# Opening stage of a two-layer AdaLN block: gates broadcast through DRAM, rows turned back into their own buffers, 64-column modulation matmuls, another batch order

## The chip, the core and the metric

The kernel runs on one core of a Trainium2 chip. The core has a matrix engine (TensorE; its matmuls are "PE" and its weight loads "PEld" in the profile), a vector engine (VectorE, DVE), an activation engine (ScalarE, ACT), a general engine (GpSimd, POOL) and a queue processor (SyncE, SP). Each engine executes its own instructions in their order and waits on semaphores for the others. Data lie in an on-chip memory of 128 partitions (SBUF), matmul results in an accumulator memory (PSUM), of which this kernel uses eight banks in three pools of 3, 2 and 3. Transfers between DRAM and SBUF are issued by an engine's queue (SPq, ACTq, POOLq) and carried out by DMA engines.

The metric is device time in microseconds, the median of several runs. The profile is one further execution.

## What is computed

Two layers, each with two branches. A branch normalises its input, scales and shifts it by values that depend on the batch (the modulation), applies an operator, and adds the result times a gate to the input. Batch 4, sequence 1024, width 256, all fp32. Cut to what matters here, layer 0:

```python
mod = (_silu(L0_c) @ L0_wmod).reshape(L0_c.shape[0], 6, 1, -1)
sa, ca, ga, sb, cb, gb = (mod[:, 0], mod[:, 1], mod[:, 2], mod[:, 3], mod[:, 4], mod[:, 5])
ga = (2 * (ga >= 0) - 1) * jnp.maximum(jnp.abs(ga), 0.25)
gb = (2 * (gb >= 0) - 1) * jnp.maximum(jnp.abs(gb), 0.25)
h = _layernorm(x, axis=-1) * (1 + ca) + sa
x = x + ga * _L0_attn_ref(h, L0_attn_queries, L0_attn_combiners)
h = _layernorm(x, axis=-1) * (1 + cb) + sb
x = x + gb * _L0_ffn_ref(h, L0_ffn_W1, ...)
```

The attention has no softmax and four heads of 64. Per head and batch it is `h (Q (h^T h) C)`, so that it can be computed from the 64 x 64 Gram matrix `h^T h` of each head:

```python
Q = jnp.einsum('btae,aeqf->qbtaf', x, qw)
pre = jnp.einsum('qbtaf,buqf->qbtau', Q, x)
attn = jnp.einsum('qbtau,buqg->abtqg', pre, x)
out = jnp.einsum('abtk,akg->btag', attn, combiners)
```

The feed-forward part of layer 0 routes each token to the best two of eight experts. Layer 1 has a gated fast-weight product in place of the attention and a routed linear layer. They follow the stage that is changed and are not touched.

## The kernel before

The program has two recorded parts. The first is **phase A**: the attention of layer 0, the second normalisation, the router logits, and the tables that say which rows go to which expert. The rest is the expert blocks of layer 0 and all of layer 1. Phase A is written as pieces handed to a planner (`class Plan`, L39): each piece names its engine, an expected duration, what it follows, the buffers ("slots") that it holds and a rank. `Plan.run` (L61) lists them in the order of begin times that it works out, and that order becomes each engine's instruction order. So an engine's order is fixed before the run, from the planner's durations, ranks and slot counts (L858), and not by what really finishes first.

Tokens lie as `x_sb[128, 8, batch, 256]`: eight tiles of 128 tokens for each batch. A *group* is four tiles; a batch has two groups. For each batch:

* **First half** (`first_half`, L1060, at rank `FIRSTS[b]`). For each group: statistics on DVE (L942, L943), a square root on ACT (L950), a Newton step of five small DVE instructions (L954 to L961), the normalised rows `xn` on ACT (L968). PE turns them to features (`to_features`, `pm_t`, L1008); ACT applies the modulation by feature on the way out of PSUM (L1013, `h1T`). PE turns that back to tokens (`to_tokens`, `pm_b`, L1035), and ACT copies it to `h` (L1040), a buffer of its own (`h1` in this half, `h2` in the second). The Gram matrix of the batch (`pm_gram`, L1102) needs both groups of `h`. Then come two short products: DVE copies the diagonal blocks (`gd`, L1112), PE makes `pm_t1` (L1134), ACT copies it (L1144), PE makes `pm_m` (L1155), and DVE multiplies that by the gate `ga0` into `md` (L1167).
* **Second half** (`second_half`, L1183, at rank `SECONDS[b]`). PE makes the attention's output `pm_o` from `h1T` and `md` (L1195), DVE adds it to `x_sb` (L1205), and the normalisation runs again with the second modulation, giving `h2T`. PE makes the router logits `pm_l` (L1235), DVE chooses the experts (`route`, L394, L1253), PE turns `h2T` back, ACT copies it to `h`, and SP stores it to `h_rows` in DRAM (L1270), from where the expert blocks gather rows. One batch (`SPLIT`) is routed in two pieces.

**Modulation.** `mods_by_feature` (L874) makes the four shift and scale vectors with one matmul for each 128 features and half of the contraction, with four moving columns (one for each batch), from `sT`, the silu of the conditioning vector (`silu_of`, L308). The two gates are made as rows on four partitions (`gate_row`, L901). Since `ga0` and `gb0` are needed on all 128 partitions, `gates` (L917) then multiplies the rows by a selector `pick` (L250): for each batch one matmul of 4 x 512 (`spread`, L332, the instruction is L335), and two ACT copies out of PSUM (L927, L928).

**SP's queue** in phase A: the eight loads of x (L218) with the small weights between them, the first two sets of expert weights (L236, L237), a filler row of `h_rows` (L853), the second layer's modulation weights (`load_wm1`, L1307), filler rows for later tables, then the eight stores of `h_rows`. ACT's queue loads the modulation weights of layer 0.

**The end of phase A**: when all router logits are there, PE turns the choices (`turn`, L434), DVE builds the block tables (L562, L667), GpSimd gathers the first rows (L348), and the first expert matmul (L1609) starts.

Of the kernel before, what the change touches and what calls it, by code (L numbers as in the profile page):

```python
# [8 lines left out]
F32 = mybir.dt.float32  # L9
F16 = mybir.dt.float16  # L10
I32 = mybir.dt.int32
AF = mybir.ActivationFunctionType
# [11 lines left out]
E = 8  # L24
# [113 lines left out]
def adaln_d2_kernel(  # L138
# [92 lines left out]


    w1buf = [pw.tile([P, W1ROW], F32, name=f"w1_{i}") for i in range(2)]
    w2buf = [pw.tile([P, W2ROW], F32, name=f"w2_{i}") for i in range(2)]
    for i in range(2):
        nc.sync.dma_start(w1buf[i], W1[(E - 1) * P :, :])  # L236
        nc.sync.dma_start(w2buf[i], W2[(E - 1) * P :, :])  # L237

    xgbuf = [pw.tile([P, D], F32, name=f"xg_{i}") for i in range(4)]
# [7 lines left out]
    for e in range(E):  # L247
        nc.gpsimd.memset(rank[:, e : e + 1], float(E - e))

    pick = pa.tile([B, B, P], F32, name="pick", bufs=1)  # L250
    nc.gpsimd.memset(pick, 0.0)
    nc.gpsimd.affine_select(
        out=pick,
        in_=pick,
        compare_op=ALU.not_equal,
        fill=1.0,
        base=0,
        pattern=[[-1, B], [0, P]],
        channel_multiplier=1,
    )  # L260
    ones16 = const.tile([P, P], F16, name="ones16")
# [46 lines left out]
    def silu_of(layer, cT):  # L308
        sT = small.tile([P, KD, B], F32, name=f"sT{layer}")
        nc.scalar.activation(sT, cT, AF.Silu)  # L310
        return sT

    def mod_rows(sT, w, at, n):

        pr = psum(ps_2, [B, n], "pm_mod")
        for k in range(KD):
            nc.tensor.matmul(
                pr, lhsT=sT[:, k, :], rhs=w[:, k, at : at + n], start=(k == 0), stop=(k == KD - 1)
            )
        return pr  # L320

    def gate_of(dst, src, scratch):
# [7 lines left out]
        nc.vector.scalar_tensor_tensor(dst, sign, -1.0, size, ALU.add, ALU.mult)  # L330

    def spread(b, rows):  # L332

        pb = psum(ps_m, [P, rows.shape[1]], "pm_bc")
        nc.tensor.matmul(pb, lhsT=pick[:, b, :], rhs=rows, start=True, stop=True)  # L335
        return pb

# [500 lines left out]

    modT = const.tile([P, 4, KD, B], F32, name="modT")
    SA, CA, SB, CB = range(4)  # L840
# [16 lines left out]

    plan = Plan(p1=3, p2=2, pm=3, xn1=3, h1T=2, h1=1, xn2=2, h2T=2, h2=4, t1=1)  # L858
    PE, ACT, DVE, POOL = "PE", "ACT", "DVE", "POOL"
# [14 lines left out]
    def mods_by_feature(which, column, at):  # L874
        ps = plan.slot("p1")

        def mm():
            pf = tiles["modT", which] = psum(ps_1, [P, 2 * KD, B], "pm_modT")
            for i in range(2):
                for q in range(KD):  # L880
                    c = column[i] * D + q * P
                    for k in range(KD):
                        nc.tensor.matmul(
                            pf[:, i * KD + q, :],
                            lhsT=wm0[:, k, c : c + P],
                            rhs=sT0[:, k, :],
                            start=(k == 0),
                            stop=(k == KD - 1),
                        )

        def out_():
            pf = tiles["modT", which]
            nc.vector.tensor_copy(modT[:, which[0], :, :], pf[:, :KD, :])
            nc.vector.tensor_scalar(
                modT[:, which[1], :, :], pf[:, KD:, :], 1.0, None, ALU.add
            )

        i = plan(PE, 1.8, mm, holds=[ps], at=at, rank=-1)
        return plan(DVE, 0.4, out_, after=[i], holds=[ps], rank=-1)

    def gate_row(i, column, at):  # L901
# [13 lines left out]
        )  # L915

    def gates(after):  # L917
        done = []
        for b in range(B):
            ps = plan.slot("pm")  # L920

            def mm(b=b):
                tiles["spread", b] = spread(b, gate_rows.rearrange("b i d -> b (i d)"))

            def out_(b=b):
                pb = tiles["spread", b]
                nc.scalar.copy(ga0[:, b, :], pb[:, :D])  # L927
                nc.scalar.copy(gb0[:, b, :], pb[:, D:])  # L928

            m = plan(PE, 0.9, mm, after=after, holds=[ps], rank=b - 0.4)  # L930
            done.append(plan(ACT, 0.8, out_, after=[m], holds=[ps], rank=b - 0.4))
        return done

# [65 lines left out]
    def to_features(b, g, key, slot, dst, held, shift, scale, after, rank):  # L999

        done = []
        for k in range(KD):
            ps = plan.slot("pm")

            def mm(k=k):
                pt = tiles["pt", key, k] = psum(ps_m, [P, 4, P], "pm_t")
                for i in range(4):
                    nc.tensor.transpose(  # L1008
                        pt[:, i, :], tiles["xn", key][:, i, k * P : (k + 1) * P], ident
                    )  # L1010

            def out_(k=k):
                nc.scalar.activation(  # L1013
                    dst()[:, k, :, :],
                    tiles["pt", key, k],
                    AF.Identity,
                    bias=modT[:, shift, k, b : b + 1],
                    scale=modT[:, scale, k, b : b + 1],
                )

            m = plan(PE, 0.55, mm, after=after, holds=[ps, slot, held], rank=rank)
            done.append(plan(ACT, 0.67, out_, after=[m], holds=[ps, held], rank=rank))
        return done

    def to_tokens(key, src, held, dst, to, after, rank):

        done = []
        for i in range(2):
            ps = plan.slot("pm")

            def mm(i=i):
                pb = tiles["pb", key, i] = psum(ps_m, [P, 2, D], "pm_b")
                for q in range(2):
                    for k in range(KD):
                        nc.tensor.transpose(  # L1035
                            pb[:, q, k * P : (k + 1) * P], src()[:, k, 2 * i + q, :], ident
                        )

            def out_(i=i):
                nc.scalar.copy(dst()[:, 2 * i : 2 * i + 2, :], tiles["pb", key, i])  # L1040

            m = plan(PE, 0.55, mm, after=after, holds=[ps, held, to], rank=rank)
            done.append(plan(ACT, 0.6, out_, after=[m], holds=[ps, to], rank=rank))
        return done
# [12 lines left out]

    FIRSTS, SECONDS, SPLIT = [0.0, 1.89, 1.82, 2.75], [1.66, 2.89, 3.45, 2.92], 2

    def first_half(b, arrival):  # L1060

        rank = FIRSTS[b]
        held, to = plan.slot("h1T"), plan.slot("h1")
        hT = buffer(("h1T", b), "h1T", [P, KD, NC, P])
        h = buffer(("h1", b), "h1", [P, NC, D])
        whole = []
        for g in range(2):
            key, slot = (1, b, g), plan.slot("xn1")
            n = normalised(
                b, range(4 * g, 4 * g + 4), key, slot, lambda c: [], rank, arrival[g]  # L1070
# [13 lines left out]
            )  # L1084
            whole += to_tokens(
                key,
                lambda cs=cs: hT()[:, :, cs, :],
                held,
                lambda cs=cs: h()[:, cs, :],
                to,  # L1090
                f,
                rank,
            )

        ps, gd, md = plan.slot("p1"), gds[b % 2], mds[b % 2]

        def gram(j, cs):
            if j == 0 and cs[0] == 0:
                tiles["gram", b] = psum(ps_1, [P, KD, P], "pm_gram")
            for c in cs:  # L1100
                hj = h()[:, c, j * P : (j + 1) * P]
                nc.tensor.matmul(  # L1102
# [12 lines left out]
        for j in range(KD):  # L1115
            for cs in (range(4), range(4, NC)):
# [5 lines left out]
                        after=m,  # L1122
                        holds=[ps, to],
                        rank=rank,
# [38 lines left out]
        def head_m_out():  # L1163
# [12 lines left out]
            head_m_out,  # L1176
            after=[m, gates0[b], *before],
            holds=[ps],
# [4 lines left out]
    def second_half(b):  # L1183
# [34 lines left out]
        for g in range(2):  # L1218
# [25 lines left out]
            if b == SPLIT:  # L1244
                of_batch["routed"] = ready[g][0]
            h2, to = buffer(("h2", b, g), "h2", [P, 4, D]), plan.slot("h2")
            backs[g] = (to_tokens(key, hT2, held2, h2, to, f, rank + 0.1), to, h2)
        for gs in routed:
# [16 lines left out]
            for g in gs:  # L1265
                back, to, h2 = backs[g]

                def store(g=g, h2=h2):
                    at = 4 * g * B * P
# [3 lines left out]
                        )[b],  # L1273
                        h2(),
                    )

                plan("SP", 4.0, store, after=back, holds=[to], rank=rank)

# [6 lines left out]
    rows_done = [gate_row(0, 2, 10.0), gate_row(1, 5, 12.0)]  # L1285
    gates0 = gates(rows_done)
    for b in range(B):
# [21 lines left out]

    loaded = plan("SP", 0.3, load_wm1, after=[mods_a, mods_b, *rows_done])  # L1310
    for piece in range(3):
        ps = plan.slot("p2")
        m = loaded
        for k in range(KD):

            def mm(piece=piece, k=k):
                if k == 0:
                    tiles["rows1", piece] = psum(ps_2, [B, 2 * D], "pm_mod")
                nc.tensor.matmul(
                    tiles["rows1", piece],  # L1320
                    lhsT=sT1[:, k, :],
                    rhs=tiles["wm1"][:, k, 2 * D * piece : 2 * D * (piece + 1)],
# [1145 lines left out]
```

## Time and profile before

| | us |
|---|---|
| runs, median of 3 | 1163.62 |
| runs, lowest and highest | 1161.59, 1166.54 |
| profiled execution, its own time | 1162.08 |
| its span, first to last instruction | 1160.3 |
| first Gram copy (L1112) starts | 33.51 |
| last router call of phase A (L1235) ends | 110.42 |
| first expert matmul (L1609) starts | 126.32 |

The span is the part of the profiled execution between its first and last instruction; 1.8 us lie around it. "Busy" is the time in which an engine had an instruction under way. For PE it says nothing of how fast: the granted clock of PE stands beside it, 1.00 being full speed. Its mean over this execution is 0.984. An instruction's row gives start, length, engine, line, operation, output and inputs, their shapes, how many were merged into the row, and, in brackets, how long the engine stood idle before it and what released it. A matmul of fp32 operands appears as two records, an fp32 transpose as one.

### The profile page before, as it was taken

The page shows a single profiled execution, that of the slowest core. Times are in us where ns is not written, and L with a number is a line of the kernel's source. Part 1 is how long each engine was busy: PE and PEld are TensorE (multiplying, and loading weights), DVE is VectorE, ACT ScalarE, POOL GpSimd, SP SyncE. Part 2 cuts the span into 40 slices and gives each one's busy share as a digit, 9 for nine tenths or more (in the row PEclk, how much of TensorE's full clock was granted, in tenths as well). Part 3 has the DMA queues.
Part 4 walks back from the last instruction along what each step waited for, and adds up shares of the span by engine and source line. Part 5 has one row for each costly group of instructions (what it writes and reads, how often), then busy time and mean ns, then how long its engine had stood idle before and what let it go on. Part 6 is the DMA issues. An engine that isn't in the chain of part 4 may idle for free. (4 is left out here: it accounts for less than half of the span.)

```text
span 1160.3 us, 18416 instructions
## 1 busy us (share of the span) xinstructions
PE 1109.2 (96%) x6244; PEld 875.8 (75%) x6244; DVE 586.3 (51%) x2243; ACT 427.4 (37%) x1156; POOL 412.1 (36%) x479
## 2 busy tenths in 40 slices
PE   9999899999999999999989999999999999999893
PEld 5997799999999999999978455665657676646651
DVE  6686333322222222222244589878587535787566
ACT  4967233223233333333224333423324325342421
POOL 2000344444333344334464452420124332545544
PEclk7999999999999999999998999999999999999997
DMA  9203323655431415151251211110013323332534
GB/s 342 107 31 110 140 80 110 223 174 186 152 126 50 175 38 191 37 178 51 70 190 51 64 56 55 55 37 19 0 37 103 111 71 98 105 122 91 142 103 129
DMA packets 78305, 122.13 MB, mean 105 GB/s; under 512 B 23610, under 2 KB 62016, under 8 KB 73604
## 3 DMA queue, kind: packets, MB, share of 16 engines
q0 software_dynamic: 31680, 69.61, 19.3%
q1 hardware_dynamic: 45428, 49.75, 12.7%
q10 hardware_dynamic: 1104, 1.58, 0.4%
q8 instruction: 52, 0.85, 0.3%
q14 instruction: 41, 0.34, 0.1%
HBM read 204.13 MB, written 30.57 MB: 202 GB/s over the span
## 5 line engine op out<-in xcount | busy, mean ns | idle before, releaser
L1621 ACT ACTIVATE hid<-p_h,w 128x128 f32<-128x128 f32 x544 | 155.1, 368 | 339.6 <-issue 266.6
L1609 PEld LDWEIGHTS p_h<-xT,w 128*128 128x128 f32 x2176 | 255.3, 193 | 7.1 <-DVE xT L1594 3.3
L1609 PE MATMUL p_h<-xT,w 128*128 128x128 f32 x2176 | 256.8, 277 | 3.5 <-DVE xT L1594 2.9
L1632 PE MATMUL p_y<-w,hid 128*128 128x256 f32 x1088 | 252.1, 384 | 3.2 <-issue 3.2
L1906 PE MATMUL p_u<-hT,a 128*128 128x512 f32 x512 | 230.9, 595 | 1.7 <-issue 1.0
L348 POOL DMA_INDIRECT w<-in_W,g_wrow x134 | 133.8, 998 | 271.4 <-ACT hid L1621 130.3
L1632 PEld LDWEIGHTS p_y<-w,hid 128*128 128x128 f32 x1088 | 203.0, 192 | 29.4 <-issue 4.4
L1906 PEld LDWEIGHTS p_u<-hT,a 128*128 128x128 f32 x512 | 94.2, 190 | 98.2 <-issue 90.6
L1594 DVE COPY xT<-pm_x 128x256 f32<-128x256 f32 x68 | 28.8, 424 | 187.3 <-PE pm_x L1589 176.5
L1954 PE MATMUL p_f<-a,hf 128*128 128x256 f32 x512 | 116.6, 380 | 2.4 <-DVE step L1995 1.6
L1643 DVE TENSOR_TENSOR y<-p_y,w 128x256 f32<-128x256 f32 x68 | 28.8, 424 | 176.4 <-PE p_y L1632 176.4
L348 POOL DMA_INDIRECT xg<-h_rows,g_row x68 | 65.7, 966 | 130.9 <-DVE g_hits L752 110.5
L1954 PEld LDWEIGHTS p_f<-a,hf 128*128 128x128 f32 x512 | 95.9, 190 | 20.8 <-issue 5.9
L348 POOL DMA_INDIRECT yg<-y,g_slot x64 | 61.3, 959 | 85.9 <-DVE x_sb L1466 33.5
L2215 PE MATMUL p_e<-ew,xT 128*128 x280 | 70.3, 384 | 0.3 <-ACT y L2225 0.3
L348 POOL DMA_INDIRECT xg<-ga_rows,ga_row x39 | 37.2, 954 | 91.6 <-DVE ga_row L761 35.0
L1918 ACT ACTIVATE hf<-p_u,decay 128x512 f32<-128x512 f32 x56 | 38.0, 683 | 72.3 <-PE p_u L1906 68.2
L2215 PEld LDWEIGHTS p_e<-ew,xT 128*128 128x128 f32 x280 | 49.5, 190 | 10.4 <-issue 4.9
L1529 DVE TENSOR_TENSOR h<-h,mod 128x256 f32<-128x256 f32 x128 | 51.4, 425 | 9.2 <-ACT h L1519 6.3
L1922 DVE SCALAR_TENSOR_TENSOR hf<-p_u,decay,hf 128x512 f32<-128x512 f32 x56 | 41.9, 748 | 20.9 <-PE p_u L1906 13.4
L2225 ACT COPY y<-p_e 128x256 f32<-128x256 f32 x70 | 25.9, 371 | 57.0 <-PE p_e L2215 24.3
L2002 POOL TENSOR_TENSOR x_sb<-x_sb,step 128x256 f32<-128x256 f32 x32 | 23.8, 743 | 62.1 <-DVE step L1995 44.5
(368 smaller groups left out, 1296.8 us busy)
## 6 DMA issues: line engine op xcount, KB each, us to landing
y<-y SPq DMA_DIRECT2D x68, 128.0 KB
ga_y<-y SPq DMA_DIRECT2D x39, 128.0 KB
x_sb<-in_x SPq DMA_DIRECT2D x8, 512.0 KB
h_rows<-h SPq DMA_DIRECT2D x8, 512.0 KB
gb_y<-y SPq DMA_DIRECT2D x31, 128.0 KB
out_x<-x_sb SPq DMA_DIRECT2D x7, 512.0 KB
a<-in_fw SPq DMA_DIRECT2D x6, 512.0 KB
mod<-mod_rows SPq DMA_DIRECT2D x6, 512.0 KB
```

The source lines that it names most:

```text
L348: return nc.gpsimd.indirect_dma_start(out=dst, out_offset=None, in_=table, in_offset=bass.IndirectOffsetOnAxis(ap=index, axis=0), bounds_c ...
L1529: nc.vector.tensor_tensor(h, h, mods1[(sc, sh)[i]][:, b, :], (ALU.mult, ALU.add)[i])
L1594: nc.vector.tensor_copy(xT, pt)
L1609: nc.tensor.matmul(p1[:, i, :], lhsT=w1[:, k * H + m * P : k * H + (m + 1) * P], rhs=xT[:, k, :], start=(k == 0), stop=(k == KD - 1),)
L1621: nc.scalar.activation(hid[:, m, :], p1[:, i, :], AF.Relu, bias=w1buf[j % 2][:, KD * H + m : KD * H + m + 1],)
L1632: nc.tensor.matmul(p2, lhsT=hid[:, m, :], rhs=w2[:, m * D : (m + 1) * D], start=(m == 0), stop=(m == KH - 1),)
L1643: nc.vector.tensor_tensor(y, p2, w2buf[j % 2][:, KH * D :], ALU.add)
L1906: nc.tensor.matmul(pu, lhsT=a[:, k, m * P : (m + 1) * P], rhs=made["n1", c, "hT"][:, k, :, :], start=(k == 0), stop=(k == KD - 1),)
L1918: nc.scalar.activation(made[key, m], made[key, m, 0], AF.Silu, scale=decays[c])
L1922: nc.vector.scalar_tensor_tensor(h, made[key, m, 1], decays[c], h, ALU.mult, ALU.mult)
L1954: nc.tensor.matmul(made[key, "p2", b], lhsT=made[key, m][:, b * P : (b + 1) * P], rhs=a1[:, m, :], start=(m == 0), stop=(m == KH - 1),)
L2215: nc.tensor.matmul(made[key, "p2"], lhsT=made[key, "xT"][:, k, :], rhs=ew_flat[:, bass.ds(made[key, "at"] + k * D, D)], start=(k == 0), st ...
```

## The change

It has four parts, all in phase A. (a) The gate rows are no longer multiplied by a selector: SP stores the four gate rows to a small DRAM tensor `gates0` and loads them back with the same row for all partitions, first `ga0`, and later `gb0`. The loads of the expert weights, which stood ahead of the plan, become a piece of the plan behind the load of `ga0`, and the second layer's modulation weights come behind them. In the built SP queue, the first of the four weight loads stands between the store and the load of `ga0`, the other three behind it, then `gb0`. (b) The rows turned back to tokens are written into the `xn` buffer that they came from, and the `h1` and `h2` buffers go; `xn1` has five buffers in place of three, `xn2` six in place of two. (c) `sT` is padded with zeros to 64 columns and the modulation matmuls of `mods_by_feature` move all 64; the four that matter are read. (d) The ranks of the batches' halves change, and the batch that is routed in two pieces is 3 in place of 2.

```diff
-    for i in range(2):
-        nc.sync.dma_start(w1buf[i], W1[(E - 1) * P :, :])
-        nc.sync.dma_start(w2buf[i], W2[(E - 1) * P :, :])
...
-    pick = pa.tile([B, B, P], F32, name="pick", bufs=1)
-    nc.gpsimd.memset(pick, 0.0)
-    nc.gpsimd.affine_select(
...
     def silu_of(layer, cT):
-        sT = small.tile([P, KD, B], F32, name=f"sT{layer}")
-        nc.scalar.activation(sT, cT, AF.Silu)
+        sT = pa.tile([P, KD, ROUTER], F32, name=f"sT{layer}", bufs=1)
+        nc.vector.memset(sT, 0.0)
+        nc.scalar.activation(sT[:, :, :B], cT, AF.Silu)
         return sT
...
-    modT = const.tile([P, 4, KD, B], F32, name="modT")
+    modT = const.tile([P, 4, B, KD], F32, name="modT")
+    gates0 = dram.tile([B, 2, D], F32, name="gates0")
...
-    plan = Plan(p1=3, p2=2, pm=3, xn1=3, h1T=2, h1=1, xn2=2, h2T=2, h2=4, t1=1)
+    plan = Plan(p1=3, p2=2, pm=3, xn1=5, h1T=2, xn2=6, h2T=2, t1=1)
...
-            pf = tiles["modT", which] = psum(ps_1, [P, 2 * KD, B], "pm_modT")
+            pf = tiles["modT", which] = psum(ps_1, [P, 2 * KD, ROUTER], "pm_modT")
...
-    def gates(after):
-        done = []
-        for b in range(B):
-            ps = plan.slot("pm")
-
-            def mm(b=b):
-                tiles["spread", b] = spread(b, gate_rows.rearrange("b i d -> b (i d)"))
-
-            def out_(b=b):
-                pb = tiles["spread", b]
-                nc.scalar.copy(ga0[:, b, :], pb[:, :D])
-                nc.scalar.copy(gb0[:, b, :], pb[:, D:])
...
             def out_(i=i):
-                nc.scalar.copy(dst()[:, 2 * i : 2 * i + 2, :], tiles["pb", key, i])
+                nc.scalar.copy(tiles["xn", key][:, 2 * i : 2 * i + 2, :], tiles["pb", key, i])
...
-    FIRSTS, SECONDS, SPLIT = [0.0, 1.89, 1.82, 2.75], [1.66, 2.89, 3.45, 2.92], 2
+    FIRSTS, SECONDS, SPLIT = [0.0, 1.27, 2.12, 2.24], [1.14, 3.78, 2.27, 3.07], 3
...
-                hj = h()[:, c, j * P : (j + 1) * P]
+                hj = tiles["xn", (1, b, c // 4)][:, c % 4, j * P : (j + 1) * P]
...
-            after=[m, gates0[b], *before],
+            after=[m, gate_loaded, *before],
...
-    gates0 = gates(rows_done)
+
+    def gates_out():
+        nc.sync.dma_start(gates0, gate_rows)
+
+    def gate_in(i, dst):
+        nc.sync.dma_start(dst, gates0[:, i, :].partition_broadcast(P))
+
+    q = plan("SP", 0.1, gates_out, after=rows_done, rank=-0.8, lag=2.2)
+    gate_loaded = plan("SP", 0.1, lambda: gate_in(0, ga0), after=[q], rank=-0.8, lag=3.5)
+
+    def first_weights():
+
+        for i in range(2):
+            nc.sync.dma_start(w1buf[i], W1[(E - 1) * P :, :])
+            nc.sync.dma_start(w2buf[i], W2[(E - 1) * P :, :])
+        gate_in(1, gb0)
+
+    weights0 = plan("SP", 0.5, first_weights, after=[gate_loaded])
...
-    loaded = plan("SP", 0.3, load_wm1, after=[mods_a, mods_b, *rows_done])
+    loaded = plan("SP", 0.3, load_wm1, after=[weights0])
```

## The prediction

> **What bounds the kernel now.** First the page's busy table: TensorE (PE) is busy for 96% of the span, so the question is what its busy time is made of in the stretch that the change touches, the opening attention stage ("phase A"), which ends where the first expert matmul starts.
>
> ```profile
> PE 1109.2 (96%) x6244; PEld 875.8 (75%) x6244; DVE 586.3 (51%) x2243; ACT 427.4 (37%) x1156; POOL 412.1 (36%) x479
> ...
> 126.32 3.81 PE L1609 MATMUL p_h<-xT,w 128*128 128x128 f32 x32 [0.56 <-DVE gb_both L390]
> ```
>
> So at most the first 126 us can change. Each engine's instruction order behind that point is the same in both builds, apart from line numbers, so whatever phase A gains should arrive at the end undiluted. Next, phase A cut into stretches (us; per engine busy time and instruction count for PE, PEld, DVE, ACT, POOL; then granted PE clock, DMA share, GB/s):
>
> ```profile
> 14.00:17.30 3.30, 3.30 (x12) 1.82 (x10) 2.96 (x15) 1.27 (x3) 0.00 (x0) 0.51 1.13 320
> 17.30:20.80 3.50, 3.12 (x14) 1.63 (x13) 3.28 (x13) 3.50 (x9) 0.00 (x0) 0.98 1.13 365
> 20.80:31.00 10.20, 10.19 (x33) 6.50 (x32) 6.92 (x35) 6.11 (x16) 0.00 (x0) 0.50 1.01 417
> 31.00:92.20 61.20, 60.33 (x543) 56.62 (x542) 47.75 (x186) 49.33 (x100) 0.00 (x0) 1.00 0.15 52
> 92.20:110.40 18.20, 15.97 (x133) 14.24 (x133) 9.52 (x48) 13.74 (x25) 0.00 (x0) 1.00 0.42 145
> ```
>
> A busy PE hides two things: from 20.8 to 31 it is busy at half clock, and the last stretch has gaps. Then the timeline, line by line (start, length, engine, line), in the front:
>
> ```profile
> 17.87 1.09 PE L335 MATMUL pm_bc<-gate_rows,pick 4*128 4x512 f32 x2 [0.38 <-DVE gate_rows L330]
> 18.89 1.10 PE L1035 MATMUL pm_b<-ident,h1T 128*128 128x128 f32 x8
> 19.92 3.06 PE L335 MATMUL pm_bc<-gate_rows,pick 4*128 4x512 f32 x4
> 22.91 1.97 PE L1008 MATMUL pm_t<-ident,xn 128*128 128x128 f32 x8
> ...
> 28.66 4.81 PE L1102 MATMUL pm_gram<-h 128*128 128x128 f32 x32
> ...
> 33.51 0.59 DVE L1112 COPY gd<-pm_gram 64x128 f32<-64x128 f32 x2 [0.56 <-PE pm_gram L1102]
> ```
>
> The gate spreads (L335) stand in PE's queue between the turns that batch 0's Gram matrix waits for; the same transposes take 1.04 us at full clock and 1.97 here. In the tail it is a different picture:
>
> ```profile
> 97.11 1.14 PE L1008 MATMUL pm_t<-ident,xn 128*128 128x128 f32 x8 [0.21 <-ACT h L1040]
> ...
> 97.80 1.45 ACT L1013 ACTIVATE h2T<-pm_t,modT 128x512 f32<-128x512 f32 x2 [0.27 <-PE pm_t L1008]
> 99.14 2.07 ACT L968 ACTIVATE xn<-x_sb,ln_m,ln_y 128x256 f32<-128x256 f32 x4
> 101.10 1.05 ACT L1040 COPY h<-pm_b 128x512 f32<-128x512 f32 x2
> 101.72 1.14 PE L1008 MATMUL pm_t<-ident,xn 128*128 128x128 f32 x8 [0.21 <-ACT h L1040]
> ```
>
> ScalarE (ACT) needs 1.45 + 2.07 + 1.05 = 4.57 us for a group of four token tiles; PE's turns repeat every 4.61 us (97.11 to 101.72) though PE has only 0.88 + 0.88 + 1.78 = 3.54 of work for one. ACT paces the tail, and only because the groups come one by one.
>
> **The change, part by part.** I use pitches (start to next start) at full clock: eight transposes 0.88, one Gram matrix 3.57, four output matmuls (pm_o) 0.89, a router call (pm_l) 1.78, pm_t1 0.95, pm_m 0.66.
>
> *Front, to the first Gram copy (33.51 now).* Removed: four spreads, 6.2 us of busy PE as they ran (one at full clock took 1.09), and eight ACT copies of 0.37 = 2.9 us. Without them the chain runs: pm_b(0,0) at 18.4 (its h1T ends at 18.3, and today it waits behind a spread until 18.9); h copies to 20.35; last xn to 20.85; pm_t(0,1) at 21 (today 22.91, behind two spreads); h1T to 23; pm_b to 24; Gram 24 to 27.6 at full clock. VectorE (DVE) is then the later one. Between the gate rows (finished 17.72) and the Gram copy its new queue holds 16 statistics pairs of 0.53 (8.5), four variance adds of 0.2 (0.8) and two five-step Newton groups of 0.97 (1.9) = 11.2 us, so the copy cannot start before 28.9; today the queue holds one pair and one Newton group more and 2.6 us of waits. With small waits I take 29.5: 4.0 earlier. At half clock throughout, pm_t and pm_b take 2.0 each and the Gram about 4.7: copy at 30.6, 2.9 earlier. **I take 3.8**; ends 2.9 and 4.6.
>
> *Clock: rule against row.* The Trainium skill ("TensorE: Matmul & The Clock Gate", part 4, PE-mode transpose) says that transposes do not count as PE work for the clock gate. That speaks against this change: with the spreads gone, PE has only transposes from 16 to 24 us, the clock would stay at half through the Gram, and the copy comes at 30.6 (gain 2.9). The row: with the spreads in place the clock was 0.50 from 20.8 to 31.0 all the same, and it rose only when the Gram ran; full-length spreads on 4 partitions did not hold it. So removing them loses little, and I lean to the upper half. What may help is the modulation matmul at 64 columns: 16 records of 4 columns take 1.84 to 1.95 us today, 16 records of 64 columns (pm_l) 1.95, since the weight load (1.9 us) sets both. Cost 0 to 0.1 us per call, and the array moves sixteen times the columns in it. Only if the clock stays full from 14 to 31 does it pay; that is in the 4.6.
>
> *Gates through DRAM.* Added on SP: an 8 KB store that waits for the gate rows, then a 512 KB load. Behind that store SP now holds the first W1/W2 loads (4.36 MB), the second layer's modulation weights (1.5 MB) and filler rows. No row shows a landing time. The skill ("DMA: Bandwidth & Descriptors", anatomy of one DMA) gives about 2 us of fixed cost per transfer. Of the first 6.4 MB (x, the layer's modulation weights, small ones) the 5-us stretches had moved 4.4 MB by 15 us; the rest at 347 GB/s ends about 20.7. So my estimate is: store landed about 22.5, the 1.05 MB load ahead until 23.7, gates 1.4 us of data at 380 GB/s plus 2: **ga0 about 27**. Its reader, md (L1167 today), stands in DVE's queue behind two Newton groups and three pairs at about 33.3: cover 6 us, cost nothing. Without cover every us of lateness is a us, because md blocks DVE's queue (the residual adds and statistics behind it, and pm_o on PE). W1/W2 would land near 33, needed at 126; wm1 near 39, needed past 100; gb0 much later. All hidden. pick's two POOL steps (1.1 us) and two added DVE memsets (0.17 each, inside its 3.26 us wait for x) cost nothing.
>
> *Middle, from batch 0's pm_t1 (34.20) to batch 3's (79.39).* Same instructions, rows copied back into xn, other batch order. By pitches PE has 42.2 us of work in today's 45.2: waits 3.0. In the new order 43.1 us of work lie before that point. I walked the DVE queue with the rows' pitches (statistics 0.53, variance add 0.2, residual add 0.69, Newton 0.97, routing of eight tiles 3.6). From md (33.3 to 33.9) to the second Gram copy stand 2 Newton, 10 statistics, 4 adds, 2 variance adds = 10.4: copy at 44.3, against 47.56. To the third: second md at 48, one Newton, then the routing waits for batch 0's router call, 53.9 by PE's queue, and ends at 57.6; 3 adds, 5 statistics, one Newton, one variance add = 5.9: 63.5, against 65.65. To the fourth: third Gram and md done at 67.2, 6.4 of DVE, but the fourth Gram ends on PE at 74.6: copy at 74.7, against 78.75. One pm_o later pm_t1 starts at 75.5, waits 45.9 - 43.1 = 2.8. So the middle keeps the front's gain.
>
> *Tail, from batch 3's pm_t1 to the end of the last router call (110.42).* Today 26.4 us of work in 31.0: waits 4.6. In the new order 25.5 us of PE work and 24.2 us by ACT (22.4 to the last h2T, then a router call). Six xn2 buffers let the turns run ahead of the copies, and eight turns back stand before the last router call where today PE waited 0.51 + 0.23. Walking PE and ACT together I find six waits of 0.3 to 0.6, **2.8 in all: 1.8 saved**. Behind it the routing of the last group, the two turns and the block tables are unchanged (15.9 us).
>
> Sum: 3.8 + 0.2 + 1.8 = 5.8. Profiled execution 1162.08 (span 1160.3 + 1.8 around it) - 5.8 = **1156.3**. That execution lies 1.5 below the median of the runs shown (1163.62), and those spread over 5 us; I predict 1156.3 and let the range take the offset.
>
> **Rivals.**
> - *Hidden anyway* (gain about 2, 1160): the front's gain only moves the wait to DVE, which is busy 90% from 17 to 25 us and paces all of the walk above; short handoffs of 0.1 to 0.2 that my walk leaves out add up. For it: my third Gram copy is only 2 us early. Against: 1.75 us more PE work is done by then.
> - *More than I see* (gain 10 to 11, 1151.5): clock full throughout (4.6) and PE without waits behind it (7.6 today) would give up to 12. Against: ACT is within 1.3 us of PE in the tail.
> - *Slower*: the gate load lands late. If its data goes behind all W1/W2, wm1 and filler bytes issued by SP (6.3 MB, 16.6 us at 380 GB/s from 20.7), it lands at 20.7 + 16.6 + 1.4 + 2 = 41; then md runs at 41 against 37.48 today, +3.5, less the tail's 1.8 = 1163.8, and over 0.5% slower only from about 45. It decides from landing at about 39. Against: ga0 is issued before three of the four weight loads.
> - *Not as said*: the new order could lose its depth, xn1 being held until the Gram has read it; five buffers for batches of two groups show no such wait in the walk. It would be the first rival.
>
> **Chances.** Forecast 0.64 (own range 1152.5 to 1160), hidden 0.18, more 0.12, slower 0.06. What this measurement can tell from no change is 0.5%, 5.8 us: below 1157.8 is faster. That is four fifths of the forecast case and all of "more": 0.64; slower by over 0.5% is about 0.05; the rest 0.31. The range 1151.5 to 1161.5 leaves out the slower case and the edges.
>
> **What would show it.** Right: no L335 rows; first Gram copy at 29 to 30.6; md not released by DMA; batch 3's pm_t1 near 75 to 76; the last router call ending at 104 to 105; the first expert matmul at 120 to 121. Wrong: md's idle time ended by a DMA; the clock at 0.50 past 31; PE waiting for ACT in the tail every group as now; a different time behind the first expert matmul.

## The result and the profile after

| | before | after |
|---|---|---|
| median of 7 runs each, us | 1163.62 (1157.9 to 1166.54) | 1154.62 (1152.36 to 1156.61) |
| ratio, 95% interval | | 0.9926 (0.9901 to 0.9951) |
| profiled execution, own time / span | 1162.08 / 1160.3 | 1154.62 / 1152.6 |
| first Gram copy starts | 33.51 | 29.94 |
| batch 0's pm_t1 starts | 34.20 | 30.64 |
| batch 3's pm_t1 starts | 79.39 | 76.13 |
| last router call ends | 110.42 | 103.54 |
| first expert matmul starts | 126.32 | 119.45 |
| from there to the span's end | 1033.98 | 1033.15 |

The three runs of before shown ahead of the prediction are among the seven; the profiled execution of after is one of its seven, and happens to be the median. The change is faster by 9.0 us between medians and by 7.46 us between the two profiled executions. 6.87 of these 7.46 us are there when the first expert matmul starts. In three steps, each the length of a stretch in one profile against the other: 3.56 up to batch 0's pm_t1 (3.57 in the Gram copy), -0.30 from there to batch 3's pm_t1 (45.19 to 45.49), 3.62 from there to the last router call (31.03 to 27.41); the 15.9 us behind that are the same.

The stretches of the profile after, cut at the same times as before (per engine busy time and count for PE, PEld, DVE, ACT, POOL; then clock, DMA share, GB/s):

```profile
14.00:17.30 3.30, 1.97 (x12) 1.04 (x12) 3.01 (x15) 0.75 (x3) 0.00 (x0) 1.00 1.12 317
17.30:20.80 3.50, 1.64 (x11) 1.24 (x11) 3.26 (x13) 3.50 (x8) 0.00 (x0) 0.98 1.13 362
20.80:31.00 10.20, 9.42 (x55) 8.64 (x56) 8.71 (x42) 7.99 (x18) 0.00 (x0) 0.67 0.97 358
31.00:92.20 61.20, 59.91 (x551) 57.34 (x550) 47.53 (x189) 49.99 (x98) 0.00 (x0) 1.00 0.27 96
92.20:103.60 11.40, 10.64 (x93) 10.03 (x93) 8.18 (x41) 9.58 (x19) 0.00 (x0) 1.00 0.29 95
```

Two readings. From 14 to 20.8 us PE is busy for 3.61 us where it was busy for 6.42: with the spreads gone, it waits for ACT. And from 20.8 to 31 it does 55 records where it did 33, in the same 10.2 us: five of the 33 were spreads, which took 4.25 us there, and the clock is now 0.67 and not 0.50. The timeline of the front after, of PE, DVE and SP's queue:

```profile
18.28 0.24 SPq L1249 DMA_DIRECT2D gates<-gate_rows  x1
...
18.75 0.99 PE L1004 MATMUL pm_b<-ident,h1T 128*128 128x128 f32 x7 [0.34 <-ACT h1T L982]
...
21.18 1.33 PE L977 MATMUL pm_t<-ident,xn 128*128 128x128 f32 x5 [1.12 <-ACT xn L937]
...
22.09 0.38 SPq L1252 DMA_DIRECT2D ga<-gates  x1
...
24.93 4.97 PE L1063 MATMUL pm_gram<-xn 128*128 128x128 f32 x32
...
29.94 0.59 DVE L1073 COPY gd<-pm_gram 64x128 f32<-64x128 f32 x2 [0.58 <-PE pm_gram L1063]
...
34.25 0.59 DVE L1128 TENSOR_TENSOR md<-pm_m,ga 64x128 f32<-64x128 f32 x2
```

The brackets tell the story. PE's turns now wait for ACT (`h1T`, `xn`) and no longer stand behind a spread. The copy still waits for the Gram matrix, which took 4.97 us, 2.6 of them at half clock (at full clock it takes about 3.6). But DVE waits only 0.58 us for it: its own queue of statistics, which the prediction took for the bound, ends at 29.36. The last row has no bracket: DVE came to `md` without a wait, so the gate load, issued 12.2 us before, was not late.

The tail after, PE alone:

```profile
92.34 1.04 PE L1004 MATMUL pm_b<-ident,h2T 128*128 128x128 f32 x8
94.02 0.66 PE L977 MATMUL pm_t<-ident,xn 128*128 128x128 f32 x4 [0.65 <-ACT h2T L982]
94.52 1.90 PE L1196 MATMUL pm_l<-wr_sb,h2T 128*128 128x64 f32 x16
...
96.69 1.04 PE L1004 MATMUL pm_b<-ident,h2T 128*128 128x128 f32 x8
97.56 2.21 PE L1196 MATMUL pm_l<-wr_sb,h2T 128*128 128x64 f32 x16
99.61 1.04 PE L977 MATMUL pm_t<-ident,xn 128*128 128x128 f32 x8
100.49 1.26 PE L1004 MATMUL pm_b<-ident,h2T 128*128 128x128 f32 x8
101.59 1.95 PE L1196 MATMUL pm_l<-wr_sb,h2T 128*128 128x64 f32 x16
```

Behind the row at 94.02, whose 0.65 us is the one wait with a bracket in this tail, there is none: each router call has a turn of another group ahead of it, in place of a wait for ACT. From batch 3's pm_t1 to the end of the last router call PE was busy for 28.76 of 31.03 us before, and for 26.56 of 27.41 us now.

### The profile page after: what moved, and what is told of

Its sections match the earlier page's. It is cut to its first block, busy times and chain, and to the rows that moved or that the text cites. A ratio compares the mean times of both kernels' runs of the same rounds, so it can differ in the third digit from the quotient of the medians.

```text
span 1152.6 us, 18406 instructions
## 1 busy us (share of the span) xinstructions
PE 1100.8 (96%) x6236; PEld 872.3 (76%) x6236; DVE 586.6 (51%) x2245; ACT 425.1 (37%) x1148; POOL 410.6 (36%) x477
```

## The experiments

Two theories stood against each other. *By parts*: each of the four parts has its own place and its own gain, and they add up. *Together*: the front's gain belongs to the gates alone, and the tail's gain comes only when buffers and order fit each other. Beside them stood the question whether the clock, by way of the 64 columns or the spreads, does the work. The kernels of one group ran on one chip, against runs of the kernel before on that chip. The chips differ: the stretch behind the first expert matmul takes 1034 us on the chip of the result and 1015 to 1019 us on the others, so times are compared within a group and landmarks across. The ratios are those on record, with their intervals; they are not the quotients of the medians beside them.

### The kernel before with one part of the change

Gates alone:

```diff
-    gates0 = gates(rows_done)
+    q = plan("SP", 0.1, gates_out, after=rows_done, rank=-0.8, lag=2.2)
+    gate_loaded = plan("SP", 0.1, lambda: gate_in(0, ga0), after=[q], rank=-0.8, lag=3.5)
...
+    weights0 = plan("SP", 0.5, first_weights, after=[gate_loaded])
```

With the spreads go their eight ACT copies and the selector, and the expert weights move behind the gates on SP's queue; these were not taken apart.

> The kernel before with the gates through DRAM alone. Theory (the gain comes from the front, freed of the spreads, and from the tail, freed by buffers and order): first Gram copy at 29.5 to 31 (33.5 before), first expert matmul at 122 to 123.5 (126.3 before), ratio 0.997. Rival (the PE clock is what counts, so the columns do it): first Gram copy no earlier than 32.5, first expert matmul at 125.5 or later. Rival (all of the gain is the batch order): the front is earlier but the first expert matmul is at 125.5 or later.

Columns alone:

```diff
-        sT = small.tile([P, KD, B], F32, name=f"sT{layer}")
-        nc.scalar.activation(sT, cT, AF.Silu)
+        sT = pa.tile([P, KD, ROUTER], F32, name=f"sT{layer}", bufs=1)
+        nc.vector.memset(sT, 0.0)
+        nc.scalar.activation(sT[:, :, :B], cT, AF.Silu)
...
-            pf = tiles["modT", which] = psum(ps_1, [P, 2 * KD, B], "pm_modT")
+            pf = tiles["modT", which] = psum(ps_1, [P, 2 * KD, ROUTER], "pm_modT")
```

> The kernel before with the 64-column modulation matmuls alone. Theory: the clock stays full from 14 to 17.3 but falls later, since ScalarE and VectorE pace that stretch; first Gram copy within 0.7 of 33.5, first expert matmul within 1 of 126.3, ratio 0.999 to 1.001. Rival (clock): full clock through the Gram matrix, first Gram copy at 31 or earlier, first expert matmul at 124.3 or earlier.

Buffers alone:

```diff
-    plan = Plan(p1=3, p2=2, pm=3, xn1=3, h1T=2, h1=1, xn2=2, h2T=2, h2=4, t1=1)
+    plan = Plan(p1=3, p2=2, pm=3, xn1=5, h1T=2, xn2=6, h2T=2, t1=1)
...
-                nc.scalar.copy(dst()[:, 2 * i : 2 * i + 2, :], tiles["pb", key, i])
+                nc.scalar.copy(tiles["xn", key][:, 2 * i : 2 * i + 2, :], tiles["pb", key, i])
```

> The kernel before with rows going back to their own buffers (and the new slot counts) alone. Theory: front as before (first Gram copy 33 to 34), tail 1 to 2.5 us shorter: last router call ends at 108 to 109.5 (110.4 before), first expert matmul at 124 to 125.3. Rival (all of the gain is the batch order): first expert matmul within 0.7 of 126.3.

Order alone:

```diff
-    FIRSTS, SECONDS, SPLIT = [0.0, 1.89, 1.82, 2.75], [1.66, 2.89, 3.45, 2.92], 2
+    FIRSTS, SECONDS, SPLIT = [0.0, 1.27, 2.12, 2.24], [1.14, 3.78, 2.27, 3.07], 3
```

> The kernel before with the new batch ranks alone. Theory: without the buffers the order helps little, first expert matmul at 125 to 127. Rival (all of the gain is the batch order): first expert matmul at 122 or earlier, with the tail's waits of PE (4.6 us from batch 3's second short product to the last router call) halved.

Measured, with the landmarks of one profile for each (the tail is the stretch from batch 3's pm_t1 to the end of the last router call):

| | time, us | ratio, 95% interval | first Gram copy | tail | first expert matmul |
|---|---|---|---|---|---|
| before, this chip | 1147.89 | | | | |
| gates alone | 1143.62 | 0.9957 (0.9942 to 0.9972) | 30.82 | 31.08 | 124.12 |
| columns alone | 1148.09 | 1.0001 (0.999 to 1.0012) | 35.10 | 31.03 | 127.94 |
| buffers alone | 1145.73 | 0.9977 (0.9969 to 0.9984) | 35.82 | 29.68 | 127.23 |
| order alone | 1148.73 | 1.0005 (0.9994 to 1.0015) | 35.65 | 30.57 | 128.13 |

Gates alone move the front and leave the tail as it was (31.03 before). Buffers alone shorten the tail by 1.35 and leave the front. Order alone takes 0.46 off the tail, which the time does not show, and columns alone do nothing. The four ratios fall by 0.43, -0.01, 0.23 and -0.05 per cent, 0.60 in all; the whole change gave 0.74 on the first chip and 0.83 in its repetition below. That difference is within the intervals and decides nothing. The tails do: 0 + 0 + 1.35 + 0.46 is 1.8 us, and the whole change has 3.62. They repeat closely: 31.03 in both profiles of before, 27.41 and 27.42 in the two of the changed kernel.

In the tail of the kernel with the buffers alone, PE's last router call still waits for ACT:

```profile
109.56 1.77 PE L1227 MATMUL pm_l<-wr_sb,h2T 128*128 128x64 f32 x14 [0.85 <-ACT h2T L1013]
```

### The kernel before, profiled again

> The kernel before once more, for its landmarks on this chip: how far the front moves from one profiled execution to the next. Theory (the half-clock windows fall where they will): first Gram copy between 33 and 36, first expert matmul between 126 and 128.3, and the tail from the fourth first-product to the last router call within 0.3 of 31.0. Rival (the front is the same in every execution): first Gram copy within 0.3 of 33.5.

The three parts that keep the spreads all had later fronts than the profile of before from which the prediction was made, and so missed the landmarks that were expected of them. The first expert matmul of gates alone was late as well, and its time better than expected. So the same kernel was profiled once more, with no edit. Its first Gram copy came at 35.40 and its first expert matmul at 128.22, each 1.9 us later than in the first profile, with the same middle (45.20) and tail (31.03). PE in its front:

```profile
17.72 2.07 PE L335 MATMUL pm_bc<-gate_rows,pick 4*128 4x512 f32 x2
19.72 1.97 PE L1035 MATMUL pm_b<-ident,h1T 128*128 128x128 f32 x8
21.62 3.78 PE L335 MATMUL pm_bc<-gate_rows,pick 4*128 4x512 f32 x4
```

The first spread takes 2.07 us and the eight turns 1.97; in the first profile they took 1.09 and 1.10. There the clock was full from 18 to 20 us; here it is at half from 12 to 32. PE is busy for 24.29 of the 24.30 us from 11 to 35.3, so here the spreads' time in its queue lies on the path, whatever their ACT copies cost. So the first profile of before shows a lucky front beside this one (35.10 to 35.82 in the three parts that keep the spreads), and a profile is one draw of it.

### The changed kernel with one part undone

Each is the changed kernel with the edit above taken back: the spreads in place of the store and the load; separate `h` buffers; the old ranks.

> The changed kernel with the spreads put back, everything else changed. Theory: it loses the front, 3.5 to 4.5 us, and keeps the tail; first Gram copy 33 to 36, first expert matmul 123 to 125.5, ratio to before 0.996 to 0.998. Rival (buffers and order carry it, the gates are hidden): ratio 0.994 or lower.

> The changed kernel with the old buffers and slot counts. Theory: it keeps the front and loses most of the tail; tail from the fourth first-product to the last router call 29.5 to 31, ratio 0.995 to 0.997. Rival (the order alone makes the tail): tail 28 or less, ratio 0.9935 or lower.

> The changed kernel with the old batch ranks. Theory: buffers with the old order give about half of the tail's gain; tail 29 to 30, ratio 0.9935 to 0.996. Rival (the order is worth nothing beside the buffers): ratio within 0.001 of the full change's on this chip or 0.993 and lower, tail 27.5 to 28.

| | time, us | ratio, 95% interval | first Gram copy | tail | first expert matmul |
|---|---|---|---|---|---|
| before, this chip | 1146.19 | | 35.40 | 31.03 | 128.22 |
| gates undone | 1145.33 | 1.0005 (0.9993 to 1.0017) | 34.91 | 30.85 | 127.79 |
| buffers undone | 1139.68 | 0.9939 (0.9919 to 0.9958) | 28.51 | 29.72 | 120.28 |
| order undone | 1140.28 | 0.9947 (0.993 to 0.9965) | 29.54 | 29.67 | 121.59 |

With the buffers or the order undone, the tail is 29.7 and the front stays early. So the last 2.3 us of the tail (29.7 to 27.41) need both: this is shown from both sides. The time of the kernel without the new buffers came out better than expected (0.995 to 0.997).

With the gates undone, the expectation missed. It gave the tail's gain to this kernel, and there is none: 30.85, and a time equal to that of before. The planner lays out the whole of phase A anew when the front's pieces change, and with the new ranks and the spreads, ACT's last groups wait for DVE. One such row of ACT in that tail:

```profile
101.17 2.08 ACT L973 ACTIVATE xn<-x_sb,ln_m,ln_y 128x256 f32<-128x256 f32 x4 [1.03 <-DVE ln_m L966]
```

So with the spreads in place the buffers alone give 29.68, the order alone 30.57, and both 30.85: the 27.41 needs the gates' part as well. What in the planner's list brings the statistics so late there was not followed further.

### The clock, the columns and the gate load

Four kernels on one chip. First the changed kernel once more, as the mark for the others, with no edit:

> The changed kernel once more, for its landmarks and its ratio on this chip. Theory: first Gram copy 29 to 31, tail within 0.3 of 27.4, first expert matmul 119 to 120.5; against a front of the kernel before that mostly runs at half clock (35.4) this is 7 to 9 us, ratio 0.992 to 0.994. Rival (the wide difference of the medians was chance): ratio 0.9945 to 0.996.

Then with four modulation columns in place of 64 (the columns' edit taken back):

> The changed kernel with modulation matmuls of four columns. Theory: the clock falls to half by 14 and stays there until the Gram matrix, which ends 0.5 to 1.5 us later: first Gram copy 30 to 31.5, ratio 0.0005 to 0.0015 above the full change's. Rival (the columns are worth nothing once the spreads are gone): first Gram copy within 0.3 of 29.9, ratio the same within 0.0005.

Then with 13 matmuls of 512 fp16 columns, which add to nothing that is read, in PE's idle time in batch 0's front, to hold the clock:

```diff
+            if b == 0:
+                kept_busy(1.6 if g == 0 else 0.5, n, rank + 0.01)
             whole += to_tokens(key, slot, lambda cs=cs: hT()[:, :, cs, :], held, f, rank)
+            if b == 0 and g == 0:
+                kept_busy(1.0, f, rank + 0.01)
```

> The changed kernel with 13 fp16 matmuls of 512 columns on ones put into PE's idle time in the front, their results unused. Theory: the clock stays full through the Gram matrix, the first Gram copy comes at 28 to 28.8 where VectorE's queue allows it, 1 us before the changed kernel's; ratio 0.991 to 0.993. Rival (VectorE's queue is the bound, the clock costs nothing): first Gram copy at 29.3 or later. Rival (fillers delay the chain): first Gram copy at 30.5 or later.

Last, with the load of `ga0` issued behind the expert weights, `gb0` and the second layer's modulation weights, while the planner still takes it for early, so that the instruction order of the engines stays:

```diff
-    gate_loaded = plan("SP", 0.1, lambda: gate_in(0, ga0), after=[q], rank=-0.8, lag=3.5)
...
-    weights0 = plan("SP", 0.5, first_weights, after=[gate_loaded])
+    weights0 = plan("SP", 0.5, first_weights, after=[q])
+
+    def load_wm1():
+        tiles["wm1"] = load_mod(wmod1, nc.sync)
+        gate_in(0, ga0)
+
+    loaded = plan("SP", 0.3, load_wm1, after=[weights0])
+    gate_loaded = weights0
```

> The changed kernel with the load of ga0 moved behind all weight loads and the second layer's modulation weights on SP's queue. Theory: the load lands at 39 to 42, the first gate product waits for it and blocks VectorE's queue, and the whole of phase A moves: first gate product 39 to 42 (34.3), first expert matmul 124 to 127 (119.5). Rival (there is slack behind the product): first expert matmul at 122 or earlier.

| | time, us | ratio, 95% interval | first Gram copy | md | tail | first expert matmul |
|---|---|---|---|---|---|---|
| before, this chip | 1148.02 | | | | | |
| changed kernel again | 1138.49 | 0.9917 (0.989 to 0.9945) | 29.06 | 33.37 | 27.42 | 118.57 |
| four columns | 1137.23 | 0.9916 (0.9888 to 0.9945) | 28.54 | 32.82 | 27.42 | 118.03 |
| filled | 1135.61 | 0.9907 (0.9877 to 0.9937) | 28.48 | 32.75 | 27.41 | 117.95 |
| gate load late | 1146.98 (one run) | | 29.38 | 40.44 | 27.41 | 127.93 |

*Columns.* Undoing them costs nothing that shows, against what was expected: the Gram copy came at 28.54, 0.5 earlier than with 64, and the ratios are the same. They do change the clock, in all 14 profiles of this study. In the six profiles with four columns it fell to half between 11.6 and 13.9 us; in seven with 64 between 18.7 and 20.7, and in the eighth, the filled one below, not at all. But this stretch does not decide: the second turns and the Gram matrix lie behind it. There the clock was at half, for a part at least, in all seven with 64, and in five of the six with four; in this one it was full from 16.6 us on. That is one draw: of the four runs of this kernel, two had a mean clock of only 0.984 and 0.986, where the profiled one had 0.990.

*Clock.* In the filled kernel it was 1.00 from the start to 35 us. The rows around its Gram copy, then the copy with four columns and that of the changed kernel again:

```profile
28.38 0.18 DVE L912 BATCH_NORM_AGGREGATE ln_mv<-ln_st 128x2 f32<-128x6 f32 x1
28.48 0.56 DVE L1077 COPY gd<-pm_gram 64x128 f32<-64x128 f32 x2
29.14 1.10 PE L1099 MATMUL pm_t<-comb,gd 128*128 128x256 f32 x4 [1.45 <-issue]
...
28.54 0.56 DVE L1072 COPY gd<-pm_gram 64x128 f32<-64x128 f32 x2
...
29.06 0.59 DVE L1073 COPY gd<-pm_gram 64x128 f32<-64x128 f32 x2 [0.60 <-PE pm_gram L1063]
```

The filled copy has no bracket and starts where the statistics before it end; it is PE that stands idle now, until the copy is there. So with PE out of the way DVE's own queue holds the copy at 28.5, and the same is seen with four columns, where the clock was full as well. In the changed kernel as it is, the clock costs what DVE stands idle before the copy: 0.58 us in the profile of the result and 0.60 in this one. That the former has its copy at 29.94 and this one at 29.06 is not the clock: there DVE began the same queue 0.9 us later (the gate rows ended at 18.25 and at 17.35, with the clock still full in both). The filled kernel has the lowest median, but its interval overlaps that of the changed kernel, so it is not shown to be faster. Its profiled execution is shorter by 3.47 us, of which only 0.62 are there at the first expert matmul.

*Late gates.* SP's queue, DVE and PE around the wait, in the timeline of this kernel:

```profile
29.77 0.86 SPq L1252 DMA_DIRECT2D ga<-gates  x1
...
40.44 0.59 DVE L1128 TENSOR_TENSOR md<-pm_m,ga 64x128 f32<-64x128 f32 x2 [6.78 <-DMA ga<-gates]
...
41.18 3.75 PE L1156 MATMUL pm_o<-md,h1T 128*128 128x128 f32 x16 [7.44 <-DVE md L1128]
```

Here is what a gate load that is not covered looks like: DVE stands 6.78 us for the DMA, and PE 7.44 us for DVE. `md` is 7.07 later than in the changed kernel on this chip, but the first expert matmul is 9.36 later. The rest is in the windows (columns as above):

```profile
37.00:41.00 4.00, 0.00 (x0) 0.00 (x0) 0.54 (x2) 0.00 (x0) 0.00 (x0) 0.50 0.72 225
41.00:44.00 3.00, 2.82 (x13) 2.85 (x14) 2.08 (x10) 0.00 (x0) 0.00 (x0) 0.50 0.00 1
```

PE stood still, the clock fell to half at 36.6 us, and stayed there up to 46.8, for the first 5.6 us of the work behind the wait; the 16 output matmuls took 3.75 us, where those of the changed kernel took 2.02 in the profile of the result:

```profile
34.99 2.02 PE L1156 MATMUL pm_o<-md,h1T 128*128 128x128 f32 x16 [0.69 <-DVE md L1128]
```

So a microsecond of lateness cost 9.36 / 7.07 = 1.3 us in this one execution. The 2.3 us more than the lateness are close to what 5.6 us at half clock cost, 2.8.

## Why the prediction was right, step by step

**Front, 3.8 (measured 3.57).** Right. Of its branches, the one at half clock throughout (30.6) is met by the gates alone, at half clock from 12 to 28.7 us: 30.82. The one with DVE's queue as the bound (not before 28.9) is met by the filled kernel: 28.48, behind gate rows that ended at 17.45. The changed kernel came at 29.94 for two reasons: its gate rows ended at 18.25 and not 17.72, from where the 11.1 us of DVE's queue lead to 29.36, and DVE then waited 0.58 us for a Gram matrix that was in part at half clock. So DVE's queue was the bound, as the prediction said, and the clock behind it worth little. What removed the time was the gates' part: it alone moved the front, and with it undone the front was late again. That it did so by the spreads' place in PE's queue is read from the second profile of before, where PE has no idle time in the front; no run took the spreads away and left their ACT copies.

**Clock, rule against row.** The prediction leaned to the row, against the rule that transposes don't count as PE work for the clock gate (the Trainium skill, "TensorE: Matmul & The Clock Gate", part 4, PE-mode transpose; the figures beside it there are of bf16 transposes, these are fp32). The row was the better guide to the sum: the spreads held nothing, and the second profile of before has them at half clock. The rule itself does not fit one profile here. In the kernel with four columns, PE had only transposes from 15.5 to 23.3 us, with gaps (its windows, one us each):

```profile
16.00:17.00 1.00, 1.00 (x7) 0.85 (x5) 0.93 (x3) 0.96 (x2) 0.00 (x0) 0.71 1.09 345
17.00:18.00 1.00, 0.42 (x2) 0.14 (x1) 0.93 (x5) 1.00 (x3) 0.00 (x0) 1.00 1.11 350
...
22.00:23.00 1.00, 0.66 (x6) 0.56 (x6) 0.90 (x6) 0.92 (x3) 0.00 (x0) 1.00 0.95 386
```

The 0.71 of the first row is half clock up to about 16.6 us and full behind it, and it stayed full through the 6.7 us of transposes that were left. The rise itself can be owed to the gate-row matmuls, which ended at 15.6; the holding hardly. In the changed kernel the same transposes saw it fall at 20.7. Which work the gate counts is left open by these runs. The columns' cost of nothing was right; their benefit, which the prediction put into the upper end, is not there in the time.

**Gates through DRAM, no cost.** Right: `md` is not released by a DMA. The estimate for the late landing in the rival, 41, compares with 40.44. The cover of 6 us was counted from an estimated landing at 27, and no row of the changed kernel shows the landing; the late load shows only that `md` has to wait when it comes behind everything. Of the store a little more is seen: SP stood from 18.94 to 22.09 ahead of the load, which needs it landed, where the estimate was 22.5. The 2 us that the estimate takes for a transfer are, in the section that it names, a fit for transfers issued by GpSimd; these are issued by SP, and no run measures that cost apart.

**Middle, waits 3.0 to 2.8 (measured 2.4).** Right in kind: the Gram copies were put at 44.3, 63.5 and 74.7 and came at 45.04, 63.94 and 75.44. One step of the working doesn't fit the other terms. A length of 45.9 up to 75.5 has pm_t1 start at 29.6; the front's 3.8 has it start at 30.4, from where the same walk gives 45.1. So the sum is 0.8 us slower than the walk that it was made from, which would have the last router call end at 75.5 + 28.3 = 103.8. It ended at 103.54, ahead of the 104 to 105 that the prediction named, and the first expert matmul at 119.45 was ahead of its 120 to 121. The 103.8 comes so close by some luck: batch 3's pm_t1 came 0.6 later than the walk had it, and the tail was 0.9 shorter.

**Tail, waits 4.6 to 2.8.** This is the term that was mis-sized. They fell to 1.9 (27.41 less 25.5 of work): 2.7 saved, not 1.8. The walk took six waits of 0.3 to 0.6 for what the profile has as one of 0.65 and a number that are too short for a bracket. The reasons given, buffers that let turns run ahead and turns laid before the last router call, hold, and they are two halves of one thing: with the gates' part in place, either without the other leaves 29.7. That the tail hangs on the gates' part too (30.85 without it) was in no step of the prediction.

**The sum.** The terms missed by -0.2 (front), +0.4 (middle) and +0.9 (tail); another 0.6 us lies behind the first expert matmul and around the span, in instructions that the change leaves alone. Predicted 1156.3; the profiled execution, which is the median run, is 1154.62. That the medians are 9.0 apart, and not 5.8, has probably a second reason, which no step of the prediction held: the profile of before had an early front, at 33.51 where the second profile shows 35.40. With that one as the base, the front gives 5.5 to 6.3 us. These are two draws on two chips, and how often each comes is not known. The prediction saw that the profiled execution was below the median and left it to the range.

**Rivals.** *Hidden*: fell, as the front's gain reached the end. *More*: the clock stayed full in the filled kernel, and from 16.6 us on in that with four columns; in both DVE's queue took over as the bound, which was worth 0.6 us. *Slower*: the mechanism is real, and its price is higher than one for one. *Not as said*: fell with `xn1`, of which no wait shows.

## What to carry to other kernels

Small matmuls that only spread a row over partitions stand in PE's in-order queue like any other work: where they sit ahead of the turns that the first result waits for, a DRAM round trip whose load was issued 12 us before its reader cost nothing here, and one that was not covered cost more than its lateness, as PE's clock fell while it waited. A planner's ranks and its buffer counts belong together, and with what is planned ahead of them: trying one part alone says little of the whole. Before a clock is blamed, look how long the reader really stood idle: here it was 0.6 us. And before a profile is used as the base for a sum, look where its throttled stretch falls, or take a second one.

## What the runs showed of the hardware

* The half-clock stretch falls differently in each execution of one kernel: 13.9 to 17.3 and 20.7 to 30.9 in the first profile of before, 12 to 32 in the second, with the Gram copy 1.9 us apart. The seven runs of before spread over 8.6 us. On two other chips, with 43 and 29 runs of before, the longer runs are those with the lower mean clock (correlation -0.60 and -0.76). But the front is not all of it: with the same instructions behind the first expert matmul, four profiles on one chip took 1015.41 to 1018.82 us there.
* Sixteen times the columns in the modulation matmuls held the clock about six microseconds longer (half from 18.7 to 20.7 us on in seven profiles, from 11.6 to 13.9 in six), at nearly the same length of the instructions: 16 records took 2.00 us in the changed kernel and 1.95 before.
* In a wait of PE of 7.4 us the clock fell to half 2.9 us after PE's last work, and stayed there for the first 5.6 us of the work behind it (0.50 up to 46.8).
* Chips differ: the same instructions behind the first expert matmul took 1034 us on one and 1015 to 1019 on three others; the two profiles of before, with 1034 and 1018 us there, have mean clocks of 0.984 and 0.983.
